# Ranked rows, fewer neighbour places and program order in the gathering layer of a four-layer graph-attention kernel, and row factors from one matmul

## The chip, the cores and the metric

The kernel runs on one core of a Trainium2 chip. The metric is device time of one execution in microseconds (us), the median over several executions. The profile is one execution on the chip, recorded by the hardware profiler. Engines are called as in the profile: PE is TensorE, DVE is VectorE, ACT is ScalarE, POOL is GpSimd, SP issues DMAs.

The kernel before took 4312 us in the runs in which the change was timed, and 4519 to 4527 us on the two chips where the experiments ran (called chip 2 and chip 13 here).

A run is called slow when it is over 1.5% above the fastest run of the same kernel, else fast. Ratios are of fast runs alone; where a median holds slow runs, the mean of the fast ones is given beside it.

## The reference

Four graph-attention layers on 3327 nodes with 256 features, each with a residual and a layer norm. Most of the change is in layer 0: its score is not separable, so every pair of neighbours needs 256 elementwise operations.

```python
def _L0_gnn_ref(nodes, adj_mat, W_src_w, W_src_b, W_tgt_w, W_tgt_b, a_w):
    g_src = nodes @ W_src_w.T + W_src_b
    g_tgt = nodes @ W_tgt_w.T + W_tgt_b
    g = leaky_relu(g_src[:, None, :] + g_tgt[None, :, :], 0.2)
    score = einsum('ijc,c->ij', g, a_w)
    score = where(adj_mat != 0, score, -inf)
    return softmax(score, axis=1) @ g_tgt
# x = layernorm(x + L0(x)), then three layers whose scores are s1[i] + s2[j]
```

The adjacency has about 1% ones, so a row has some 32 neighbours on average, and up to 56 are provided for.

## The kernel before

Nodes lie in 26 tiles of 128 rows; the last tile has 127. For each tile, DVE finds the column numbers of up to 56 neighbours a row (`neighbours`), POOL gathers one neighbour's projected row per node and place (128 rows in one indirect DMA), DVE scores, ACT turns each weight into a diagonal matrix, and PE adds diagonal times rows up.

```python
# layer 0, per tile `it` (cut)
for k0 in range(0, KMAX, GROUP):                       # KMAX 56, GROUP 8
    turn = (it * (KMAX // GROUP) + k0 // GROUP) % TURNS   # 11 gather buffers
    g = gath.tile([P, GROUP, ROW], F32, tag=f"g{turn}", name="g")
    for s in range(GROUP):
        nc.gpsimd.indirect_dma_start(
            out=g[:, s, :], in_=table_d[:, :],
            in_offset=bass.IndirectOffsetOnAxis(ap=index[:, k0 + s : k0 + s + 1], axis=0), ...)
    ...
    nc.vector.tensor_tensor(y, g[:, part : part + 4, :dim], h[it]..., op=ALU.max)
    nc.vector.scalar_tensor_tensor(y[:, s, :], y[:, s, :], 1.0, a_row, ..., accum_out=sc[:, k : k + 1])
...
for k in range(KMAX):
    nc.scalar.activation(diag, ident, AF.Copy, scale=w[:, k : k + 1])
    nc.tensor.matmul(acc[:, :dim], diag, gs[k // GROUP][:, k % GROUP, :dim], ...)
nc.vector.scalar_tensor_tensor(h[it][:pn], acc[:pn, :dim], inv[:pn], xr[:pn], ...)   # write-back
```

The order of the instructions on each engine is chosen by a scheduler. The adjacency and its transpose come in by SP's queue, four pieces a tile; the transpose is cast to bf16 by ACT and stored for the later layers.

```python
nc.sync.dma_start(adj_i[:pn, : hi - lo], adj[it * P : it * P + pn, lo:hi])        # pn is 127 in tile 25
nc.sync.dma_start(turned_i[:pn, : hi - lo], adj_t[it * P : it * P + pn, lo:hi])
```

In the layers 1 to 3 a factor per row is wanted on all 128 partitions. It comes from a matmul whose weights are one column repeated 128 times, once per head (`rates_of`).

The softmax here doesn't subtract the row's maximum and nothing guards it: scores larger than these inputs give would overflow.

## Time and profile before

| | before |
|---|---|
| timed runs | 4312 us (4308 to 4321) |
| profiled span | 4526.6 us |
| first gather | 96 us |
| layer 0 ends | 2597 us |
| layers 1 to 3 | 1927 us |

The profiled span is 5% over the timed runs. This is the chain of waits of the kernel before, from 480 to 660 us: start, length, what.

```profile
490.86 5.20 DMA turned_i<-in_adj_t_dram
...
497.45 5.76 DMA turned_i<-in_adj_t_dram
...
512.21 42.24 DMA turned_i<-in_adj_t_dram
...
583.77 44.81 DMA turned_i<-in_adj_t_dram
```

The same piece of the transposed adjacency, some 400 KB, takes 5 to 6 us in a row of tiles and then suddenly 42 and 45. The groups of 500 to 700 us say which tile it is: four casts of 127 partitions, the last tile's, have 103 us of idle time before them that ended with this load.

### The profile page before, as it was taken

What the parts mean: (1) busy time and instruction counts of PE and PEld (TensorE: products, weight loads), DVE (VectorE), ACT (ScalarE), POOL (GpSimd) and SP (SyncE); (2) the same over time, 40 slices, a digit from 0 to 9 for tenths busy, and PEclk for the clock granted to TensorE, in tenths of its full rate; (3) what the DMA queues carried; (4) which work ended last, traced back from release to release, by engine and by line L of the source; (5) the groups of instructions that cost most, each with busy time, mean ns of one, the idle gap of its engine ahead of it and who ended that gap; (6) DMA issues with size and microseconds to landing.
All of it is one profiled execution on the core that took longest, in us unless ns stands there. A gap on an engine that the chain in (4) does not pass through costs nothing.

```text
span 4526.6 us, 45858 instructions
## 1 busy us (share of the span) xinstructions
PE 2766.0 (61%) x14134; PEld 1668.4 (37%) x14134; DVE 2654.7 (59%) x7548; ACT 1722.4 (38%) x3049; POOL 1594.9 (35%) x1482
## 2 busy tenths in 40 slices
PE   5134225434343344333532599999979999999997
PEld 3122122222222233221321468887733334433333
DVE  7454436485554585474736435521138777888887
ACT  1233212222221222121321334411128777787776
POOL 1776526657566666766674400000000000000000
PEclk8566556666665666665666789999979999999998
DMA  8889725545455554644563312222211111111111
GB/s 252 216 216 225 194 71 98 105 93 113 91 97 104 95 106 98 111 100 91 106 107 62 69 51 70 69 67 69 64 27 44 39 33 36 40 43 49 48 46 36
DMA packets 199258, 413.05 MB, mean 91 GB/s; under 512 B 40830, under 2 KB 125800, under 8 KB 199008
## 3 DMA queue, kind: packets, MB, share of 16 engines
q0 software_dynamic: 69888, 193.92, 24.4%
q1 hardware_dynamic: 129120, 216.12, 15.9%
q8 instruction: 118, 1.93, 0.2%
q14 instruction: 132, 1.08, 0.1%
HBM read 380.89 MB, written 29.01 MB: 91 GB/s over the span
## 4 chain that ended last, share of the span: by engine, by line
PE 42%; DVE 18%; POOL 11%; DMA 10%; issue 9%; another core or an unknown queue 7%; ACT 2%; SPq 1%; DVEq 0%; ACTq 0%; POOLq 0%
PE acc L787 14%; POOL g L344 11%; PE acc L748 11%; PE acc L795 7%; DVE y L359 5%; DMA turned_i<-in_adj_t_dram 5%; DVE y L353 4%; PE acc L378 4%; DMA g<-table_d,index 3%; PE misc L653 3%; PE misc L614 2%; DVE cand L296 2%; DVE num L291 1%; DMA at<-at_d 1%
## 5 line engine op out<-in xcount | busy, mean ns | idle before, releaser
L344 POOL DMA_INDIRECT g<-table_d,index x1456 | 1566.9, 1076 | 960.0 <-issue 412.7
L378 PE MATMUL acc<-g,diag 128*128 128x256 f32 x2912 | 926.1, 473 | 1579.3 <-ACT diag L377 1093.2
L378 PEld LDWEIGHTS acc<-g,diag 128*128 128x128 f32 x2912 | 643.1, 233 | 1862.2 <-ACT diag L377 1158.1
L673 DVE SCALAR_TENSOR_TENSOR e<-e,at 128x896 f32<-128x896 f32 (+2 forms) x936 | 922.7, 1023 | 342.1 <-ACT e L669 285.0
L669 ACT ACTIVATE e<-rate,minus_one,feat 128x896 f32<-128x896 f32 (+2 forms) x936 | 943.2, 1070 | 249.1 <-PE acc L795 153.6
L377 ACT ACTIVATE diag<-ident,w 128x128 f32<-128x128 f32 x1456 | 532.4, 396 | 760.8 <-PE acc L378 335.4
L194 POOL TENSOR_TENSOR rstds<-rstds,minus_half 128x7 f32<-128x7 f32 (+1 forms) x16 | 24.1, 1507 | 1946.9 <-DVE rstds L193 1874.2
L787 PE MATMUL acc<-e,feat 128*64 128x384 f32 (+4 forms) x3328 | 644.6, 523 | 0.0
L359 DVE SCALAR_TENSOR_TENSOR y<-y,src 128x256 f32<-128x256 f32 x1456 | 543.0, 415 | 21.2 <-issue 8.3
L353 DVE TENSOR_TENSOR y<-g,h 128x1024 f32<-128x1024 f32 x364 | 437.0, 1217 | 111.2 <-DMA g<-table_d,index 75.7
L384 DVE SCALAR_TENSOR_TENSOR h<-acc,inv,xr 128x256 f32<-128x256 f32 (+1 forms) x26 | 12.6, 483 | 661.4 <-PE acc L378 395.8
L787 PEld LDWEIGHTS acc<-e,feat 128*64 128x64 f32 (+1 forms) x3328 | 262.9, 137 | 370.7 <-issue 207.7
L795 PE MATMUL acc<-e,feat 128*32 128x384 f32 (+4 forms) x3328 | 333.5, 518 | 0.0
L371 ACT ACTIVATE w<-scores,top 128x56 f32<-128x56 f32 x26 | 8.9, 341 | 813.8 <-DVE top L368 705.4
L748 PE MATMUL acc<-feat,e 128*128 128x257 f32 (+2 forms) x1352 | 306.9, 380 | 0.0
L748 PEld LDWEIGHTS acc<-feat,e 128*128 128x128 f32 (+2 forms) x1352 | 253.3, 190 | 36.5 <-issue 1.6
L748 PE MATMUL acc<-feat,at 128*128 128x257 bf16 (+2 forms) x2028 | 245.7, 278 | 25.5 <-DMA at<-at_d 25.5
L748 PEld LDWEIGHTS <-at 128*128 128x128 bf16 (+2 forms) x2028 | 202.5, 101 | 64.6 <-DMA at<-at_d 26.6
L304 ACT CAST turned<-turned_i 128x832 bf16<-128x832 int32 (+1 forms) x104 | 91.8, 883 | 331.5 <-DMA turned_i<-in_adj_t_dram 309.8
L296 DVE MAX8 cand<-num 128x8 f32<-128x64 f32 x1352 | 187.6, 208 | 12.5 <-issue 7.1
L795 PEld LDWEIGHTS acc<-e,feat 128*32 128x32 f32 (+1 forms) x3328 | 86.6, 108 | 226.7 <-issue 226.7
L308 DVE MAX8 found<-cand 128x8 f32<-128x416 f32 x182 | 106.7, 586 | 90.8 <-remote 59.9
(103 smaller groups left out, 1522.2 us busy)
## 6 DMA issues: line engine op xcount, KB each, us to landing
at<-at_d SPq DMA_DIRECT2D x200, 224.0 KB
turned_i<-in_adj_t_dram SPq DMA_DIRECT2D x75, 416.0 KB
adj_i<-in_adj_dram SPq DMA_DIRECT2D x75, 416.0 KB
g<-table_d,index POOLq DMA_INDIRECT x1456
at<-at_d SPq DMA_DIRECT2D x100, 192.0 KB
at<-at_d SPq DMA_DIRECT2D x100, 191.8 KB
at_d<-turned SPq DMA_DIRECT2D x75, 208.0 KB
adj_i<-in_adj_dram SPq DMA_DIRECT2D x25, 415.5 KB
```

What stands on the lines that cost most here:

```text
L296: nc.vector.max(cand[:, s * per + c, :], v[:, c * CHUNK : (c + 1) * CHUNK])
L344: nc.gpsimd.indirect_dma_start(out=g[:, s, :], out_offset=None, in_=table_d[:, :], in_offset=bass.IndirectOffsetOnAxis(ap=index[:, k0 + s ...
L353: nc.vector.tensor_tensor(y, g[:, part : part + 4, :dim], h[it][:, None, :].to_broadcast([P, 4, dim]), op=ALU.max,)
L359: nc.vector.scalar_tensor_tensor(y[:, s, :], y[:, s, :], 1.0, a_row, op0=ALU.mult, op1=ALU.mult, accum_out=sc[:, k : k + 1],)
L377: nc.scalar.activation(diag, ident, AF.Copy, scale=w[:, k : k + 1])
L378: nc.tensor.matmul(acc[:, :dim], diag, gs[k // GROUP][:, k % GROUP, :dim], start=(k == 0), stop=(k == KMAX - 1),)
L653: nc.tensor.matmul(pr[:, : hi - lo], self.w_src[:, k, h_of : h_of + 1].to_broadcast([P, P]), ht[:, k, lo:hi], start=(k == 0), stop=(k == k ...
L669: nc.scalar.activation(e[:pn, : c1 - c0], self.rate[b][:pn, h_of, : c1 - c0], AF.Relu, bias=minus_one[:pn], scale=q,)
L673: nc.vector.scalar_tensor_tensor(e[:pn, : c1 - c0], e[:pn, : c1 - c0], 1.0, at[:pn, : c1 - c0], op0=ALU.add, op1=ALU.mult,)
L748: nc.tensor.matmul(accs[s][:pn, : dim + 1], a[:pj, s * P : s * P + pn], f[:pj, : dim + 1], start=(j == 0 and part == 0), stop=(j == nt - 1 ...
L787: nc.tensor.matmul(accs[x][p][q * hd : (q + 1) * hd, : hi - lo], f[:pj, h_of * hd : (h_of + 1) * hd], es[h_of][:pj, lo:hi], start=(j == 0) ...
L795: nc.tensor.matmul(accs[x][pairs][h_of * 32 : (h_of + 1) * 32, : hi - lo], f[:pj, dim + h_of : dim + h_of + 1].to_broadcast([pj, 32]), es[ ...
```

## The change

The intent: gather less, and let no engine wait in a bad place.

1. Tiles form sets of 3, 4, 5, 7 and 7. The rows of a set are ranked by number of neighbours (a comparison with all keys of the set gives the rank, an indirect DMA scatters the lists by rank). Then only the first tile of a set needs 56 places and the others 27 to 39: 973 places in place of 1456. The node itself leaves the list and has its own gather. Results are scattered back to the original rows.
2. In layer 0, PE, DVE, ACT and POOL keep the order in which the program is written, with gathers four parts ahead of scores (a part is up to 8 places, one gather buffer) and the next set's lists worked in between.
3. The row factors of all heads come from one matmul with as many rows as heads; one row each is stored to DRAM and loaded again, spread to 128 partitions.

The core of the diff, with cuts marked and long lines abridged:

```diff
+SETS = (3, 4, 5, 7, 7)
+LEVELS = {3: (56, 36, 31), 4: (56, 37, 33, 29), 5: (56, 38, 34, 31, 28), 7: (56, 39, 36, 34, 32, 30, 27)}
...
+            s0.enter_context(tc.manual_schedule(engines={PE, DVE, Activation, Pool}))
...
+                nc.scalar.dma_start(own_d[it * P : (it + 1) * P, :], own)
...
+                    nc.vector.tensor_scalar(junk[:, : size * P], key_rows[:, : size * P], keys[:, t : t + 1], 0.0,
+                        op0=ALU.is_gt, op1=ALU.add, accum_out=ranks[:, t : t + 1])
...
+                    nc.gpsimd.indirect_dma_start(out=lists_d[s][:, :], out_offset=...ranks_i[:, t : t + 1]..., in_=payloads[t][:, :])
...
+            due.setdefault(q + 3, []).append(lambda key=key: put_back(*key))
+            for q, ((s, t), k0, _) in enumerate(parts):
+                if q + LEAD < len(parts):
+                    gather(q + LEAD)
+                score(q)
+                if q in ends:
+                    combine(*ends[q])
+                for what in due.pop(q, []):
+                    what()
+                while done < steps and done * room < (q - begun + 1) * steps:
+                    next(ahead, None)          # one step of the next set's lists
...
-            def rates_of(self, b, ht, h_of, banks):
-                            self.w_src[:, k, h_of : h_of + 1].to_broadcast([P, P]),
+            def rates_of(self, b, ht, banks):
+                            pr[: self.nh, : hi - lo], self.w_src[:, k, :], ht[:, k, lo:hi],
+                    nc.sync.dma_start(self.rate_d[: self.nh, c0 + lo : c0 + hi], row[: self.nh, : hi - lo])
+                nc.sync.dma_start(rate[:, : self.nh, : c1 - c0], rows[None].to_broadcast([P, self.nh, c1 - c0]))
```

## The prediction

> **What bounds the kernel now.** I read the page's busy shares and forty slices first, to find the stages; then the table of two stretches; then the costliest groups; then the waits of GpSimd and VectorE inside layer 0; then the chain around the end of layer 0. The busy shares and the slices of the page (rows PE to DMA, each digit tenths of a slice of 113 us):
>
> ```profile
> PE 2766.0 (61%) x14134; PEld 1668.4 (37%) x14134; DVE 2654.7 (59%) x7548; ACT 1722.4 (38%) x3049; POOL 1594.9 (35%) x1482
> ...
> PE   5134225434343344333532599999979999999997
> DVE  7454436485554585474736435521138777888887
> ...
> POOL 1776526657566666766674400000000000000000
> PEclk8566556666665666665666789999979999999998
> DMA  8889725545455554644563312222211111111111
> ```
>
> No engine is the bound over the whole span. POOL is busy in the first 23 slices and then stops: that is layer 0, the only layer that gathers. After it PE runs at 9. The timeline and chain give the edges: the first gather starts at 95.9 us, the last combining matmul ends at 2596 us, and the layers 1 to 3 take the rest. The same in the table of two stretches (length, then busy us of PE, PEld, DVE, ACT, POOL, the clock, DMA share):
>
> ```profile
> 96.00:2599.00 2503.00, 927.61 (x2918) 644.01 (x2918) 1405.68 (x5604) 618.88 (x1599) 1572.56 (x1460) 0.63 0.57 118
> 2599.00:4526.00 1927.00, 1780.94 (x11008) 981.33 (x11008) 1178.72 (x1632) 1086.38 (x1409) 18.32 (x13) 0.95 0.18 49
> ```
>
> So layer 0 is 57% of the span. Its costliest groups:
>
> ```profile
> L344 POOL DMA_INDIRECT g<-table_d,index x1456 | 1566.9, 1076 | 960.0 <-issue 412.7
> L378 PE MATMUL acc<-g,diag 128*128 128x256 f32 x2912 | 926.1, 473 | 1579.3 <-ACT diag L377 1093.2
> ...
> L359 DVE SCALAR_TENSOR_TENSOR y<-y,src 128x256 f32<-128x256 f32 x1456 | 543.0, 415 | 21.2 <-issue 8.3
> L353 DVE TENSOR_TENSOR y<-g,h 128x1024 f32<-128x1024 f32 x364 | 437.0, 1217 | 111.2 <-DMA g<-table_d,index 75.7
> ```
>
> 1456 gathers are 26 tiles of 56 places. One costs GpSimd (1566.9 + 412.7) / 1456 = **1.36 us**, with the 0.30 us between two that the waits call issue; alone, in the timeline, it repeats every 1.25 us. That is 1980 us of the 2503. The rest is in the waits of GpSimd and VectorE in 96 to 2599 us:
>
> ```profile
> POOL g L344 <- PE acc L378: 386.3, 38, 43.0
> ...
> DVE h L384 <- PE acc L378: 395.8, 12, 105.1
> DVE h L384 <- remote: 232.9, 11, 47.4
> DVE y L353 <- DMA g<-table_d,index: 75.7, 22, 7.0
> ```
>
> A tile fills 7 of the 11 gather buffers and frees none until its combining starts, so GpSimd stops for PE (386 us); VectorE, whose order the scheduler chose, sits in the write-back of a tile (629 us in two rows) while gathered rows wait for their scores. Layer 0 is thus bound by GpSimd's number of gathers, plus a ring of waits GpSimd - VectorE - ScalarE - PE - GpSimd.
>
> **What the skill says.** "GPSIMD Engine Reference", 8. Key points: indirect gathers can only be issued from GpSimd. So the number of gathers cannot be shared out; it has to fall. "Perfetto Trace Analysis", Summary: the profiler window per engine type: for such a DMA the recorded time is making the descriptors, not the movement. The trace agrees: after each record of 0.95 us or more the rows still come 2 to 7 us later (the waits of L353). "SBUF — State Buffer", Who interferes with whom: VectorE with two SBUF inputs takes a port pair that GpSimd reads through, exclusively. The trace fits: beside scoring a gather record goes from 0.95 to 1.2 to 1.9 us, mean 1.08. So with a fuller VectorE I keep 1.36 us, not 1.25.
>
> **The change part by part.**
>
> *Fewer places.* Tiles come in sets of 3, 4, 5, 7, 7. Rows of a set are ranked by number of neighbours, and only the first tile of a set gets 56 places, the others 27 to 39. Sums by set: 123, 155, 187, 254, 254 = 973 places, against 1456. The row itself leaves the list and is gathered once a tile, as its "own" row. GpSimd gets new work: 26 gathers of own rows, 26 scatters of lists, 26 scatters of results. 973 + 78 = 1051 issues. Removed: 405 x 1.36 = 551 us.
>
> *VectorE.* In a stretch where it never waits, 8 places take 5.12 us (two maxima, eight products), so 0.64 a place. Finding a tile's neighbours costs, from rows of 1000 to 2000 us over 11 tiles: 79 + 45 + 38 + 44 + about 12 = 218, so 20 us; I add 3 us for the diagonal, count, key and ranking passes. Own place, put-back and norms: 1.5 us a tile. Total 999 x 0.64 + 26 x 24.5 = 1276 us, plus about 60 of projection: about as before (1406), in a much shorter stage.
>
> *Program order on PE, VectorE, ScalarE, GpSimd.* Gathers run 4 parts ahead of scores, write-back comes 3 parts after a tile's last score. The compiled order shows it: write-back scatters stand 3 to 4 parts after the tile's own gathers. Tiles of 27 to 39 hold 4 or 5 of 11 buffers. I take the 386 us and most of the 629 us of waits as gone.
>
> But a set's gathers need the whole list of that set, so VectorE finds the next set while GpSimd gathers this one. Per set, GpSimd = (places + own + results + next lists) x 1.36; VectorE = places x 0.64 + next set x 23 + tiles x 1.5:
> - set 0: 133 issues, 181 us; VectorE 79 + 92 + 5 = 176
> - set 1: 168, 228; 99 + 115 + 6 = 220
> - set 2: 204, 277; 120 + 161 + 8 = 289
> - set 3: 275, 374; 163 + 161 + 10 = 334
> - set 4: 268, 364; 173. With VectorE half idle I take 1.33 us: 356
>
> Larger of each, summed: 181 + 228 + 289 + 374 + 356 = 1428 us.
>
> *Before the first gather.* All of the table plus the lists of three tiles. Bytes: three tiles at 4.26 MB (adjacency, its transpose, the bf16 copy) 12.8 MB, projection in and out about 20 MB (the new own table is 10.3 of it): 33 MB. At the 247 GB/s of the first 100 us that is 133 us, plus start: **150 us** against 96.
>
> *Friction, my choice.* Between sets GpSimd waits for the ranking, the scatter, the list's load and the own rows: 20 us, four times: 80. The DMA engines: a gather holds all 16 for 4526.6 x 0.244 / 1456 = 0.76 us, a tile's lists for 14 us; in set 1 that is 124 + 70 = 194 of 228 us, 85%. In slices 1 to 4 they stood at 8 to 9 and gathers slowed. I add 90 us. Tail 20.
>
> Layer 0 ends at 150 + 1428 + 80 + 90 + 20 = **1768 us**, against 2599.
>
> *Row factors.* All heads go through one matmul with as many rows as heads, one exponential, a store and a load that spreads to 128 partitions. In the last layer the old matmuls (L653) took 46 us on the path between blocks; three quarters go, 35. For the third layer they lie inside a PE-bound stage, about 50 less. Against it 8 loads of 1.8 MB beside the edge loads, DMA share 0.18: 15 us. Net **70 us**: 1857.
>
> Span 1768 + 1857 = 3625. The profile ran at 4526.6 where the timed runs gave 4314, so x 0.953: 3455. I say **3440**.
>
> **The rivals.** (a) *GpSimd alone binds and nothing else shows*: 150 + 1051 x 1.25 + 20 + 1857, times 0.953, is 3184. For it: VectorE needs less than GpSimd in four sets of five. Against it: they are within 5% in sets 0 to 2, and DMA is at 85%. (b) *VectorE in order becomes the bound*, stopped by a late adjacency load, a part that hasn't landed, or a write-back that waits for PE; each stop delays next lists too. For it: the old ACT casts waited 310 us for the transposed adjacency, and SP's queue mixes those loads with the list loads. 170 us more friction: about 3620. (c) *The gather count was hidden behind the waits*, and the waits return with the ring: layer 0 keeps its 523 us of stops and loses only 551 us: 2599 + 54 - 551 + 1857, times 0.953: 3770. Against it: shorter tiles leave six or seven free buffers.
>
> **Range and chances.** Low end nearly (a) with some boundary stalls, high end (b): 3270 to 3620. Even (c) is 12% faster, so faster by over 2% has 0.98; 0.01 each for the others.
>
> **What would show it.** GpSimd: some 1051 indirect DMAs, about 1.36 us apart, last one near 1750 us. Its waits on PE under 100 us; new waits on VectorE's ranks or on the lists at four places. VectorE over 75% busy in 150 to 1750 us, GpSimd likewise. DMA 7 to 9 in slices of that time. First gather near 150 us. Layers 1 to 3 near 1857 us, with factor matmuls a quarter as many in layer 3. It is wrong if the gather spacing goes over 1.5 us, if VectorE's waits in layer 0 stay above 400 us, if SP holds the list or adjacency loads back, or if the fallback for lost rows runs (then the time would more than double).

## The result

The changed kernel takes **3807 us** (3805 to 3808) where the kernel before takes 4312 in the same rounds: ratio 0.8826, 95% interval 0.881 to 0.884. It is correct. The ratio is the mean time of one kernel's fast runs over that of the other's of the same rounds, so it is not quite the ratio of the medians. The direction was right; the time lies outside the range (3270 to 3620).

The page after: busy shares, then tenths of 40 slices, which are now 95 us long.

```profile
PE 2286.5 (60%) x13080; PEld 1415.1 (37%) x13080; DVE 2510.1 (66%) x6859; ACT 1544.1 (41%) x2544; POOL 1152.2 (30%) x1084
...
DVE  8497695699679706554633563113678888788887
...
POOL 0376746754777602777720000000000000000000
...
DMA  8873852854377401354322222332111111211111
```

POOL is at 6 to 7 in most slices of layer 0, as hoped, but the fifteenth slice (1332 to 1427 us) is 0 for POOL, DVE and DMA alike. Something stopped the whole of layer 0 there. The two stretches and the costliest group:

```profile
150.00:1949.00 1799.00, 511.07 (x2044) 430.57 (x2044) 1235.63 (x4823) 464.93 (x1141) 1123.77 (x1051) 0.63 0.50 136
1949.00:3804.00 1855.00, 1711.16 (x10822) 936.14 (x10822) 1184.97 (x1658) 1061.26 (x1362) 20.66 (x14) 0.95 0.22 60
```

```profile
L462 POOL DMA_INDIRECT g<-table_d,lst x973 | 1030.6, 1059 | 349.5 <-issue 276.3
```

Layers 1 to 3 take 1855 us where 1857 was predicted; the first gather is at 151.6 us where 150 was predicted; the trace lists 973 gathers and three times 26 other indirect DMAs, 1051 as counted, and a gather costs (1030.6 + 276.3) / 973 = 1.34 us where 1.36 was assumed. What is off in this trace is the end of layer 0: 1949 us where 1768 was predicted. The waits of POOL and DVE from 150 to 1950 us (us in total, times, longest):

```profile
POOL lists_d L431 <- DVE ranks_i L428: 176.4, 4, 144.4
POOL sums_d L554 <- DVE hs L550: 84.8, 7, 27.5
POOL g L462 <- PE acc L540: 48.7, 24, 23.0
```

```profile
DVE num L356 <- DMA adj_i<-in_adj_dram: 226.4, 9, 112.5
DVE y L472 <- DMA g<-table_d,lst: 201.4, 76, 4.9
```

POOL's wait for PE fell from 386 to 49 us. The largest wait is a single one: 144 us for the ranks of the last set. DVE could not make them, for it waited 112.5 us for one piece of adjacency. The timeline of SP from 1280 us (start, length, engine, operation) and a table of 1340 to 1440 us show why:

```profile
1289.74 91.96 SPq L350 DMA_DIRECT2D turned_i<-in_adj_t_dram  x5
1381.80 23.61 SPq L348 DMA_DIRECT2D adj_i<-in_adj_dram  x1
```

```profile
1340.00:1440.00 100.00, 0.00 (x0) 0.00 (x0) 0.00 (x0) 3.54 (x4) 0.00 (x0) 0.50 0.07 26
```

For 100 us only four casts run. The DMA engines are busy 0.07, which is one engine of 16 (0.0625), and move 26 GB/s. These are the transfers of the last tile, with 127 rows. The Trainium skill states the reason in "DMA: Bandwidth & Descriptors", Why a DMA increments its semaphore by 16 and not by 1: the number of engines has to divide the number of rows, up to 16, so 128 rows go to 16 engines and 127 to one. The trace agrees with it. The last tile's pieces of some 380 to 445 KB, adjacency and transpose, pass one after the other: the four casts of its transpose start 23 to 24 us apart.

Two of the signs that the prediction named for being wrong are in this trace: DVE's waits in layer 0 sum to 535 us (over 400), and an adjacency load came late. DVE is busy for 69% of the stretch and POOL for 62%, not over 75%, and the DMA engines for 50%, not 70 to 90%.

### The profile page after: what moved, and what is told of

Read it like the earlier page. It is cut to its first block, busy times and chain, and to the rows that moved or that the text cites. A ratio compares the mean times of both kernels' runs of the same rounds, so it can differ in the third digit from the quotient of the medians.

```text
span 3804.9 us, 41793 instructions
## 1 busy us (share of the span) xinstructions
PE 2286.5 (60%) x13080; PEld 1415.1 (37%) x13080; DVE 2510.1 (66%) x6859; ACT 1544.1 (41%) x2544; POOL 1152.2 (30%) x1084
## 5 line engine op out<-in xcount | busy, mean ns | idle before, releaser
L462 POOL DMA_INDIRECT g<-table_d,lst x973 | 1030.6, 1059 | 349.5 <-issue 276.3
L540 PE MATMUL acc<-g,diag 128*128 128x256 f32 x1946 | 485.1, 416 | 764.2 <-ACT diag L535 732.3
L540 PEld LDWEIGHTS acc<-g,diag 128*128 128x128 f32 x1946 | 409.9, 212 | 837.7 <-ACT diag L535 773.0
L208 POOL TENSOR_TENSOR rstds<-rstds,minus_half 128x7 f32<-128x7 f32 (+4 forms) x17 | 24.3, 1432 | 1831.5 <-DVE rstds L207 1758.8
L472 DVE TENSOR_TENSOR y<-g,own_of 128x1024 f32<-128x1024 f32 (+2 forms) x250 | 298.0, 1192 | 206.9 <-DMA g<-table_d,lst 201.4
L535 ACT ACTIVATE diag<-ident,w 128x128 f32<-128x128 f32 x999 | 375.6, 398 | 55.1 <-PE acc L540 34.1
L416 PE MATMUL key_rows<-key_diag,ones 128*128 128x128 f32 x52 | 18.1, 447 | 577.2 <-DVE key_diag L415 534.3
L477 DVE SCALAR_TENSOR_TENSOR y<-y,a_row 128x256 f32<-128x256 f32 x973 | 356.4, 421 | 8.6
L375 ACT CAST turned<-turned_i 128x896 bf16<-128x896 int32 (+3 forms) x104 | 91.9, 884 | 407.3 <-DMA turned_i<-in_adj_t_dram 229.4
L356 DVE SCALAR_TENSOR_TENSOR num<-adj_i,rev 128x896 f32<-128x896 int32 (+3 forms) x104 | 105.7, 1016 | 228.2 <-DMA adj_i<-in_adj_dram 228.2
```

Of the source, the lines that this page charges most:

```text
L356: nc.vector.scalar_tensor_tensor(v[:pn, :w], adj_i[:pn, :w], 0.0, rev[:pn, lo:hi], op0=ALU.not_equal, op1=ALU.mult, accum_out=sums[:pn, b ...
L462: nc.gpsimd.indirect_dma_start(out=g[:, k - k0, :], out_offset=None, in_=table_d[:, :], in_offset=bass.IndirectOffsetOnAxis(ap=entry["lst" ...
L472: nc.vector.tensor_tensor(y[:, :m, :], rows, minus_src[:, None, :].to_broadcast([P, m, dim]), op=ALU.max,)
L477: nc.vector.scalar_tensor_tensor(y[:, i, :], y[:, i, :], 1.0, a_row, op0=ALU.mult, op1=ALU.mult, accum_out=sc[:, i : i + 1],)
L540: nc.tensor.matmul(acc[:, :dim], diag, rows, start=(k == 0), stop=(k == kt))
```

## The experiments

Twelve kernels ran, all correct. Eleven ran on chip 2, one on chip 13. The table has the median of all runs, the mean of the fast ones, the ratio to the kernel before in the same rounds with interval, and from the profile the end of layer 0 and the length of layers 1 to 3.

| run | what | median us | fast mean us | ratio to before | layer 0 ends | layers 1 to 3 |
|---|---|---|---|---|---|---|
| e1 | before | 4518 | 4518 | 0.999 (0.992 to 1.006) | 2568 | 1927 |
| e3 | before, 127 rows split | 4434 | 4434 | 0.981 (0.974 to 0.988) | 2487 | 1930 |
| e5 | after | 4080 | 4075 | 0.901 (0.896 to 0.906) | 2214 | 1861 |
| e2 | after, 127 rows split | 3977 | 3969 | 0.879 (0.874 to 0.885) | 2088 | 1862 |
| e4 | after, 8 list buffers | 4089 | 4089 | 0.904 (0.900 to 0.908) | 2235 | 1857 |
| e6 | after, both | 3982 | 3948 | none given | 2108 | 1857 |
| e7 | after, 56 places everywhere | 4698 | 4697 | 1.039 (1.035 to 1.043) | 2824 | 1856 |
| e8 | after, old row factors | 4184 | 4174 | 0.923 (0.917 to 0.928) | 2284 | 1932 |
| e9 | after, scheduler's order | 4003 | 4002 | 0.883 (0.875 to 0.890) | 2159 | 1856 |
| e10 | e2 with SP in program order | 3989 | 3980 | 0.884 (0.874 to 0.893) | 2104 | 1857 |
| e11 | e6 with edge loads split too | 3942 | 3934 | 0.874 (0.864 to 0.883) | 2084 | 1831 |
| e12 | e11 in scheduler's order (chip 13) | 3841 | 3846 | 0.853 (0.845 to 0.860) | 1995 | 1834 |

e6 had two of four runs slow and got no ratio; e2, e10 and e11 had one slow run each. The runs on chip 2 came in three sets of rounds; the fast runs of the kernel before average 4517, 4519 and 4528 us in them.

### Is the 5% between profile and timed runs a factor? (e1, e5)

Edit: none; the two kernels again.

> The kernel before, unchanged. Theory 1 (recording a profile slows the old layer 0, whose order has little slack, and not the new one): the profiled span is again near 4527 us while the timed run is near 4312. Theory 2 (the first profile of before was one odd execution): the profiled span is within 30 us of 4312, and layers 1 to 3 still take 1927 us, so that layer 0 ends near 2385 us.

> The changed kernel unchanged, on the chip of this call, as the partner of the others. Theory 1 (the first profile of before came from a chip on which layer 0 stalls often in front of single instructions; the timed runs came from another chip): where before takes about 4520 us, this takes 4060 to 4120 us and its waits named remote and issue on ScalarE, PE and VectorE in layer 0 sum to several hundred us; where before takes about 4312 us, 3800 to 3815 us and nearly none of them.

The kernel before took 4498 and 4538 us in its two runs, and the profiled span is 4496: it lies among the timed runs (4481 to 4581 in all on this chip), as the first profile does (4527). So recording a profile costs nothing here. The first profile fits the times of chip 2, and the timed runs do not; that they came from two chips is the likely reading, but the record names no chip for either. The same changed kernel now takes 4080 us in place of 3807. Its two stretches on chip 2:

```profile
150.00:2213.00 2063.00, 645.52 (x2044) 454.02 (x2044) 1239.34 (x4823) 454.40 (x1142) 1103.37 (x1051) 0.60 0.43 119
2213.00:4074.00 1861.00, 1719.70 (x10823) 938.61 (x10822) 1184.70 (x1659) 1061.80 (x1362) 20.66 (x14) 0.95 0.21 60
```

Against the stretches of the result, the layers 1 to 3 are equal (1861 and 1855). In layer 0 the busy time of DVE (1239 and 1236), of ACT (454 and 465) and of POOL (1103 and 1124) is nearly equal as well; it only takes 264 us longer. PE alone counts more, 646 us in place of 511 for the same 2044 matmuls. So a slower chip here is not one on which all work takes longer. It has more stops. The waits on chip 2 name them: ACT's and PE's, in layer 0:

```profile
ACT diag L535 <- remote: 242.6, 68, 5.9
...
ACT diag L535 <- issue: 78.8, 43, 5.2
```

```profile
PE acc L540 <- issue: 249.4, 108, 14.6
```

In the first profile of the changed kernel ACT has none for remote, and the issue waits of ACT and PE sum to under 4 us. The profile of the kernel before has them (ACT 252 us for remote in 85 pieces). They come in bursts, in which every single diagonal waits 3 to 6 us. DVE has them too (153 us for remote at its write-backs in e5). What they are is not shown: "remote" is the profile's word for a releaser that it can't name, and "issue" for an idle time in which it sees no wait. More loading of instructions is not it: those queues move the same 0.55 and 0.33 MB in layer 0 of both profiles; whether a load came late can't be seen. Their place is shown: these long waits are in layer 0.

### Did the one-engine transfers cost the 144 us? (e2, e3, e4, e6)

The edit of e2 and e3 is made at three transfers: the loads of adjacency and of its transpose, and the store of the transpose's bf16 copy. One of the three is shown. e4 is only the second hunk, and e6 is e2 with it.

```diff
+    def runs(pn):
+        return [(0, pn)] if pn == P else [(0, pn // 16 * 16), (pn // 16 * 16, pn)]      # 112 + 15
-nc.sync.dma_start(adj_i[:pn, :w], adj[it * P : it * P + pn, lo:hi])
+for r0, r1 in runs(pn):
+    nc.sync.dma_start(adj_i[r0:r1, :w], adj[it * P + r0 : it * P + r1, lo:hi])
```
```diff
-lst = io0.tile([P, KMAX + 3], U32, tag="lst", name="lst", bufs=4)
+lst = io0.tile([P, KMAX + 3], U32, tag="lst", name="lst", bufs=8)
```

> The changed kernel; only the loads of adjacency, of its transpose and the store of the bf16 copy of the last tile (127 rows) go out as two transfers of 112 and 15 rows. Theory A (a 127-row transfer runs on one of 16 DMA engines; eight of them in series stop VectorE for 112.5 us and GpSimd for 144 us at 1330 to 1480 us): 3807 falls by 110 to 150 us, to 3655 to 3700, and the stretch with 26 GB/s goes. Rival B (that stop comes from the SP queue, where a list load waits 85 us for a result scatter ahead of adjacency loads): within 25 us of 3807.

> The changed kernel with 8 buffers for the lists in place of 4, so that a list load on SP no longer waits for the result scatter of four tiles earlier (578 us of waits in 16 pieces on SP). Theory A: the long stop stays, gain 0 to 40 us. Rival B: adjacency loads come early again, VectorE's 226 us of waits for them and GpSimd's 144 us for the ranks go: 3807 falls by 100 us or more.

The expectations give 3807 as partner; on this chip it is 4080. e2 takes 3977, 103 us less than e5 and a little under the expected 110 to 150 (106 us by the means of the fast runs); the ratios 0.879 and 0.901 have intervals that do not overlap. On chip 2 the stop lies later: DVE waits 118.7 us for one piece of adjacency, and from 1550 to 1600 us the DMA engines move 26 GB/s and POOL and DVE do nothing. The slices of e5 (102 us each), then of e2 (99 us each), show it in e5's sixteenth and none like it in e2's layer 0:

```profile
DVE  7585685487838670733544355311287887888887
...
POOL 0466445545465451366673000000000000000000
...
DMA  8763742455354531134232222233211111111111
```

```profile
DVE  7486586478947687352553455211487888788887
...
POOL 0456554635375645675750000000000000000000
...
DMA  8853643365336552343322222233111112111111
```

In e2 the four casts of the last tile's transpose start 2 to 3 us apart (1474.5 to 1482.8 us), where they were 23 to 24 apart in the first trace. What is left of DVE's wait for adjacency in layer 0 and of POOL's for ranks:

```profile
DVE num L365 <- DMA adj_i<-in_adj_dram: 0.5, 1, 0.5
```

```profile
POOL lists_d L441 <- DVE ranks_i L438: 56.5, 3, 24.6
```

e4 takes 4089, so the list buffers give nothing, although SP's waits for result scatters fell from 578 us in the first trace (515 in e5) to 88 in this one; DVE still waits 117.5 us for one piece of adjacency. These were waits of an engine that was off the path. Theory A holds and rival B falls. POOL's longest wait for the ranks was 132.9 us in e5 and is 24.6 in e2; of these 108 us, 103 arrive at the end.

> The same split in the kernel before. Theory A: its two waits of 42 and 45 us on 127-row loads of the transpose at 512 and 584 us go, and GpSimd had 78 gathers in 500 to 700 us where it has 120 elsewhere: 4312 falls by 50 to 100 us. Rival (these loads lie beside a ring of waits that has its own length): within 25 us.

e3 takes 4434 where before takes 4521 in the same rounds: 1.9% less, in the expected 50 to 100 us. The long waits are gone: ACT waits for the transpose 44 us in all in 400 to 700 us, and 7.6 at most. So the kernel before paid for the same 127 rows, a little less than the one after.

> The changed kernel with the 127-row transfers of layer 0 split in 112 and 15 rows and 8 list buffers. Theory A: the split gives 110 to 150 us against the unchanged one of this call; the list buffers add 0 to 40. Rival: with the one-engine transfers gone, the list waits on SP were the next stop, and both give 200 us or more.

The two fast runs are 3929 and 3967, beside 3951 to 3992 in e2: 21 us less in the mean, which two runs cannot tell from spread; layer 0 ends no earlier in the profile. That the list buffers add anything after the split is not shown, and the rival's 200 us falls.

### Fewer gathers, or program order? (e7, e9)

e7 puts 56 places in every tile and keeps all else; e9 takes the manual order of the four engines out and keeps all else.

```diff
-LEVELS = {3: (56, 36, 31), ...}
+LEVELS = {k: (56,) * k for k in (3, 4, 5, 7)}
```
```diff
-            s0.enter_context(tc.manual_schedule(engines={PE, DVE, Activation, Pool}))
```

> The changed kernel with 56 places in every tile: ranking, sets and program order stay, 1456 gathers in place of 973 (1534 issues of GpSimd in place of 1051). Theory (number of gathers binds): 483 more at 1.34 us is 647 us, less what was stops behind VectorE (about 250): plus 350 to 500 us. Rival (program order gave the gain, the gathers were hidden): plus less than 150 us.

> The changed kernel, but layer 0 in the order that the scheduler chooses, not in program order on the four engines; places, sets and the DRAM row factors stay. On the chip of the last two calls the changed kernel takes 4080 us. Theory of the prediction (program order removes the waits in which VectorE sits at a write-back while rows wait): plus 80 to 300 us. Rival (the fewer places are all of the gain; with 56 places and program order the kernel was at 4698, slower than before): within 60 us of 4080, or faster.

e7 takes 4698 us, 618 more than e5 and more than the 350 to 500 expected. 610 of it are in layer 0, which is 1.26 us for each of the 483 places added back: nearly the whole cost of a gather on POOL, (1510.5 + 421.2) / 1456 = 1.33 us here.

```profile
L457 POOL DMA_INDIRECT g<-table_d,lst x1456 | 1510.5, 1037 | 755.0 <-issue 421.2
```

And 4698 is 3.9% slower than the kernel before, though the row factors are in it. So sets, ranking and program order together, without the fewer places, cost layer 0 some 256 us (2824 against 2568). 78 more issues of POOL at 1.33 us are 104 of that and the later first gather 54; the rest is not taken apart. Fewer places are the whole gain of layer 0 on this chip.

e9 takes 4003, 77 us *less* than e5 (73 by the means). Its ratio 0.883 (0.875 to 0.890) lies clear of 0.901 (0.896 to 0.906), in other rounds on the same chip. The theory of the prediction falls, on this chip. The waits of POOL in e5, then in e9:

```profile
POOL sums_d L554 <- DVE hs L550: 298.0, 19, 38.4
...
POOL lists_d L431 <- DVE ranks_i L428: 168.8, 3, 132.9
POOL g L462 <- PE acc L540: 117.8, 13, 35.2
```

```profile
POOL g L453 <- PE acc L531: 434.0, 23, 127.4
...
POOL sums_d L545 <- DVE hs L541: 56.1, 4, 18.7
```

In program order POOL itself stands before a result scatter until DVE has written the tile back, and no gather behind it can go. The scheduler's order has few of these waits and more for free gather buffers. The ring of waits was not removed; it changed its place. How the two orders compare on a chip without the stops is not measured.

### Does SP's order matter beside? (e10)

Edit: SP joins the engines in program order, with the split of e2.

> The changed kernel with the 127-row split and SP in program order as well, so that transposed adjacency loads no longer go out five to eight at a time ahead of the adjacency that VectorE needs next. Partner: the split alone, 3977 us on this chip. Theory (SP's order costs VectorE the other 90 us of waits for adjacency): minus 30 to 90 us. Rival (a list or result load at the head of the queue blocks more often): no gain or a loss.

3989 us against 3977, 3980 against 3969 by the fast runs: no gain. DVE's wait for adjacency had already gone in e2, and now POOL waits 106 us for list loads. The rival holds.

### The row factors (e8)

Edit: `rates_of` and its callers as in the kernel before.

> The changed kernel with the row factors as before (one matmul and one exponential a head, no trip through DRAM). Theory of the prediction: plus 55 to 85 us, all of it in layers 1 to 3 (1855 us becomes about 1927). Rival (hidden beside other work): plus less than 20 us.

4184 us, 104 more than e5 (99 by the fast runs). Layers 1 to 3 are 1932 us in place of 1861, so 71 us are the row factors, as predicted (70). The profile is of a slow run, but this stage agrees with the fast profiles of the kernel before (1927 to 1930). The rest lies in layer 0, whose code this edit does not touch, and I take it for spread; that is not tested.

### A version that beats both (e11, e12)

e11 is e6 with the 127-row split for the edge loads of layers 1 to 3 as well; e12 is e11 without the manual order.

```diff
-nc.sync.dma_start(at[:pn, : c1 - c0], at_d[j * P : j * P + pn, c0:c1])
+for r0, r1 in runs(pn):
+    nc.sync.dma_start(at[r0:r1, : c1 - c0], at_d[j * P + r0 : j * P + r1, c0:c1])
```

> The changed kernel with 8 list buffers, the 127-row split in layer 0 and also for the edge loads of layers 1 to 3 (16 loads of 190 to 224 KB that one DMA engine moves in 8 to 11 us each; the chain of layer 2 shows four of 10 to 11 us). Partner: 3981 us. Theory: layers 1 to 3 fall by 30 to 60 us. Rival (they are loaded ahead in three buffers): less than 10 us. A version to beat both kernels.

> The scheduler's order in layer 0 (4003 us alone), with the 127-row split in all layers and 8 list buffers. Theory (the gains add: about 100 us for layer 0's split, 40 for the layers'): 3850 to 3890 us, the fastest of all. Rival (the scheduler had put the last tile's loads where nothing waited for them, longest wait for adjacency 48.9 us): only the layers' 40, so 3950 to 3975 us.

e11's layers 1 to 3 are 1831 us, 26 under e6 and just short of the expected 30 to 60; in the profiles without this edit and with the new row factors they are 1855 to 1862. Its whole time says less: 3934 against 3948 by the fast runs, 14 us, which is within their spread. e12 takes 3841, ratio 0.853, below the expected 3850 to 3890 by a little, where the kernel before takes 4519. It ran on another chip than the rest, and its profile has the same stops there (ACT 206 us for remote). It is the fastest of all. That the gains add up fits the ratios (0.883 for e9, 0.853 here), though e9 ran on chip 2; the rival's 3950 to 3975 falls.

## Why the prediction was wrong

The miss is 3807 - 3440 = 367 us: 170 from a factor put on the sum, 181 from layer 0, and 15 that the prediction took off its own sum of 3455 without a reason. Step by step:

- **What bounds layer 0.** Right: the number of gathers on POOL, plus stops. e7 gives 1.26 us for each place.
- **Counts and unit costs.** Right: 1051 issues, 1.34 us against 1.36, first gather 151.6 against 150, DVE busy 1236 us after the first gather against 1276. That a gather is slower beside VectorE instructions with two SBUF inputs, as the prediction took from "SBUF — State Buffer", Who interferes with whom, is clear in the trace of the kernel before from 1000 to 2000 us: 229 gather records beside an idle VectorE last 0.95 to 0.96 us, 30 beside only its search with one input (MAX8) the same, and 38 beside only its maxima of two SBUF inputs 0.95 to 1.97, in the mean 1.47.
- **Row factors.** Right: 71 us against 70.
- **"The profile ran at 4526.6 where the timed runs gave 4314, so x 0.953."** This step failed, and is worth 3625 - 3455 = 170 us, nearly half the miss. The factor was put on everything. But e5 and the first profile of the changed kernel agree in layers 1 to 3 (1861 and 1855 us) and in the busy time of DVE, ACT and POOL, and differ by 264 us of stops in layer 0. The layers 1 to 3 (1857 us) and POOL's issues were multiplied by a factor that does not hold for them. And most of the stops had been taken out of the sum before. For the kernel before the same is inferred: it was not profiled where it took 4312 us.
- **"Friction, my choice": 80 + 90 us.** Mis-sized. Layer 0 ran 181 us over its sum (1949 against 1768). POOL's stops in it are about 370 us in the trace of the changed kernel (176 for ranks, 91 for results, 49 for PE, 33 between list scatters, 22 for landings). One of them, 144 us, was not in the sum at all: the one-engine transfers of the last tile. Its sign was in the trace before (42 and 45 us for one load), and I read past it. e2 shows that it costs 103 us on chip 2. That it costs 110 to 144 on the chip of the timed runs is an estimate from its trace, not measured. The other three waits for ranks are 32 us together, so the boundaries alone cost less than the 80 us. The 90 us for busy DMA engines had no ground: the gathers were not slower (1.34 us), at a DMA share of 0.50.
- **"I take the 386 us and most of the 629 us of waits as gone."** In the trace of the result they are: POOL waits 49 us for PE, and DVE hardly waits at write-backs. On chip 2 they are not: 118 us for PE, and 298 us for results. There program order is 77 us worse than the scheduler's (e9).
- **The rivals.** Rival (c), 3770 us, seems nearest to 3807, but only by luck: it has the factor in it, and its 523 us of stops were not there. Without the factor (c) is 3959 and rival (b) 3625 + 170 = 3795, 12 us off. Rival (b) named what came, DVE stopped by a late adjacency load so that the next lists are late. The reason it gave, the mixing of loads in SP's queue, is not what e2 and e4 show.

The 3625 without the factor and the 181 us by which layer 0 ran over make 3806, which is the profile's own sum of the two stages and so no test.

Open: what the stops named remote and issue are, why two chips have them, and what the split and the order of instructions are worth where there are none.

## What to carry to other kernels

Look at the last, uneven tile first: its transfers of 127 rows, a number with no divisor from 2 to 16, ran on one DMA engine, here at 26 GB/s, and a cut into 112 and 15 rows is a gain of 2 to 2.5% for a few lines. When profile and timed runs differ, find out in which stage and whether in work or in waits before scaling anything; a wait that has been taken out of a sum must not be scaled again. Program order on an engine is no gain in itself: a wait for a result holds up everything behind it, and on chip 2 the same kernel was faster in the scheduler's order.

## What the Trainium skill lacked or had wrong

- "DMA: Bandwidth & Descriptors", Why a DMA increments its semaphore by 16 and not by 1: right about 127 rows on one engine (busy share 0.07, one of 16). It does not say outright what follows in a kernel, that such pieces queue up one behind the other, here 23 to 24 us apart and to a stop of 112.5 us.
- No page has the spacing of indirect gathers of 128 rows: 1.33 to 1.37 us in the mean of a kernel, with 0.30 us between two records, beside a busy VectorE, in all profiles where it was worked out.
- "SBUF — State Buffer", Who interferes with whom, has no size for an indirect gather beside VectorE's instructions with two SBUF inputs: 0.95 us alone, 1.47 in the mean beside the maxima, up to 1.97.
- No page has the stops of ScalarE, PE and VectorE in front of single instructions (3 to 6 us each, together 264 us more in layer 0 for the same kernel) that two chips show while GpSimd gathers and the first profile of the changed kernel does not.
